# Two DMA queues in place of one for an activation sent across partitions, and a last tile transposed in the middle of a product

## The chip, the core and the metric

The kernel runs on one core of one Trainium2 chip. A core has a matrix engine (PE, with its weight loads shown apart as PEld), a vector engine (DVE), a scalar engine (ACT), GpSimd (POOL) and a sync engine (SP), each with its own queue of instructions. DMAs are issued from the queues of SP, ACT and POOL. The metric is the device time of one launch in microseconds, lower is better.

## The reference

A block of cross-attention with a feed-forward part, then a mixture of experts. The attention part takes 2048 tokens of 256 features as four blocks of 512 and attends to 1601 rows of context. The change is in the mixture of experts alone:

```python
router_logits = x @ wg.T                                   # 8 experts
probs = softmax(router_logits)
topk_w, topk_idx = top_k(probs, 2)
topk_w = topk_w / sum(topk_w)
...
h1 = einsum('th,eih->tei', x, w1)                          # 256 -> 512
h3 = einsum('th,eih->tei', x, w3)
y = einsum('tei,ehi->teh', silu(h1) * h3, w2)              # 512 -> 256
out = einsum('te,teh->th', expert_w, y)                    # only two experts a token count
```

## The kernel before

**The stage.** Up to about 410 us the kernel does the attention and its feed-forward part. From then on it runs the experts. Tokens have been scattered in DRAM (`slots`) into regions by expert, and the stage works through 37 tiles of 128 tokens of one expert each (`sure` is 37): 17 tiles a, 8 tiles p, 12 tiles b. All weights (`wi`, `wo`) lie in SBUF.

**One tile n**, in the loop of `run` (L1337 to L1388):

- `fetch_tile` (L1358) is called for tile n + 3. SP reads the tile's first row from a table into a register (L1149), then issues five DMAs: four for the token rows `xs` (L1155) and a small one for the tokens' weights and numbers, `at` (L1164). `xs` has four buffers.
- `turn_in` (L1189): DVE transposes `xs` in 32 x 32 blocks into `xT`. The loop does this for tile n + 2.
- `hidden` (L1207): PE makes h1 and h3, four matmul instructions each in the profile.
- ACT takes silu of h1 into `g` (L1349, for the last tile L1355), and DVE multiplies `g` by h3 (L1370, last tile L1377).
- `g` has to be transposed, so that its 512 features lie on partitions. For tiles 8 to 35 (`sent`) that takes two steps. `send_across` (L1223) issues four DMAs of 64 KB, SBUF to SBUF, each of which moves a quarter of the features of all 128 partitions into 32 partitions of `gb`. Then `turn_sent` (L1231) lets DVE transpose 32 x 32 blocks into `gT`. The other tiles, tile 36 among them, use `turn_out`: four PE transposes (L1240) and an ACT copy out of PSUM (L1242).
- `product` (L1248): PE multiplies `gT` by `wo` in four steps, eight instructions in the profile. DVE scales the rows (L1256), and POOL adds them to the output with an indirect DMA (L1258).

**Order.** On PE a tile's product comes two tiles late: the order is h1 of tile n, product of tile n - 2, h3 of tile n. From tile 8 on DVE, ACT and SP run in the order of the program text too (`by_hand`, L1341). On DVE that is: scaling of product n - 2, multiplication of tile n, transpose of `gb` of tile n - 1, transpose of `xs` of tile n + 2. On SP only fetches stand. At the end (n = 37) PE does the product of tile 35, the transposes of tile 36, and the product of tile 36. The scatters of L1258 all add to the output, and each starts after the one before it has landed.

Of the kernel before, what the change touches and what calls it, by code (L numbers as in the profile page):

```python
# [19 lines left out]
def xattn_ffn_moe(  # L20
# [21 lines left out]
    nc = tc.nc  # L42
# [11 lines left out]
    NI = I // P  # L54
# [36 lines left out]
    def bank_s(name):  # L91
        return ps_s.tile([P, 512], F32, tag="s", name=name)

    def bank_o(name):
        return ps_o.tile([P, 512], F32, tag="o", name=name)

    def bank_t(name):
        return ps_t.tile([P, 512], F32, tag="t", name=name)
# [872 lines left out]
    def spread(n, run, f, many):  # L971


        le = table(f"le{n}", [many, E])
        nc.vector.tensor_tensor(
            le,
            run.unsqueeze(1).to_broadcast([P, many, E]),
            index[:, :many].unsqueeze(2).to_broadcast([P, many, E]),
            ALU.is_le,
        )  # L980
        ex = table(f"ex{n}", [many])
        nc.vector.reduce_sum(ex, le, axis=AX.X)
        prev = summed(f"prev{n}", le, f.unsqueeze(1).to_broadcast([P, many, E]), [many, E])
        k = table(f"k{n}", [many])
        nc.vector.tensor_sub(k, index[:, :many], prev)
        return ex, k
# [159 lines left out]
    sent = range(SENT, sure - 1)  # L1146
# [49 lines left out]
    def weights_at(ex):  # L1196

        if isinstance(ex, int):
            return ex * WI, ex * WO
        return tuple(  # L1200
            nc.tensor.value_load(a, min_val=0, max_val=(E - 1) * by)
            for a, by in zip(ex, (WI, WO))
        )

    def hidden(name, xT, w, n, into):
        for c in range(ND):
            nc.tensor.matmul(  # L1207
                into,
                lhsT=xT[:, c, :],
                rhs=wi[n, c].rearrange("p e i -> p (e i)")[:, bass.ds(w[0], I)],  # L1210
                start=(c == 0),
                stop=(c == ND - 1),
            )

    def by_quarter(a):

        return a.rearrange("p (c q r) -> p q c r", q=NQ, r=Q)

    def send_across(name, g):

        gb = mp.tile([P, NQ, I // NQ], F32, tag="gb", name=f"gb_{name}")
        for q in range(NQ):
            nc.scalar.dma_start(  # L1223
                gb[q * Q : (q + 1) * Q].rearrange("t i n -> t (i n)"),
                g[:, q * (I // NQ) : (q + 1) * (I // NQ)],
            )
        return gb

    def turn_sent(name, gb):
        gT = mp.tile([P, NI, P], F32, tag="gT", name=f"gT_{name}")  # L1230
        nc.vector.transpose(  # L1231
            gT.rearrange("p c (i t) -> p i c t", t=Q),
            gb.rearrange("p i (c r) -> p i c r", r=Q),
        )
        return gT

    def turn_out(name, g):
        tp = bank_t(f"gtp_{name}")
        for i in range(NI):
            nc.tensor.transpose(tp[:, i * P : (i + 1) * P], g[:, i * P : (i + 1) * P], ident)  # L1240
        gT = mp.tile([P, NI, P], F32, tag="gT", name=f"gT_{name}")
        nc.scalar.copy(gT, tp.rearrange("p (i q) -> p i q", q=P))  # L1242
        return gT

    def product(name, at_token, gT, w, into=out):
        y = bank_o(f"y_{name}")
        for i in range(NI):
            nc.tensor.matmul(  # L1248
                y[:, :D],
                lhsT=gT[:, i, :],  # L1250
                rhs=wo[:, bass.ds(w[1] + i * D, D)],
                start=(i == 0),
                stop=(i == NI - 1),
            )
        yw = mp.tile([P, D], F32, tag="yw", name=f"yw_{name}", bufs=3)
        nc.vector.tensor_scalar_mul(yw, y[:, :D], at_token[:, 0:1])  # L1256
        added.append(
            nc.gpsimd.indirect_dma_start(  # L1258
                out=into,
                out_offset=bass.IndirectOffsetOnAxis(ap=at_token[:, 1:].bitcast(I32), axis=0),  # L1260
                in_=yw,
                in_offset=None,
                compute_op=ALU.add,
            ).ins
        )
        if len(added) in DRAINS:
            with tc.issue_after(added[-1]):
                nc.gpsimd.drain()
# [9 lines left out]
    xs, at_token, xT = {}, {}, {}  # L1278

    def fetch_tile(n):  # L1280
        if n < len(tiles):
            name, row_of, i, _ = tiles[n]
            xs[n], at_token[n] = fetch(n, name, tabs[row_of][0:1, i : i + 1])

    def turn_tile(n):
        if n < len(tiles):
            xT[n] = turn_in(tiles[n][0], xs.pop(n))

    def expert_of(n):
        if n < len(tiles):  # L1290
            _, _, i, ex = tiles[n]
            if isinstance(ex, str):
                i = 0 if ex == "exp" else i
                ex = [a[0:1, i : i + 1] for a in tabs[ex]]
            ws[n] = weights_at(ex)
# [21 lines left out]
    def between(n):  # L1317
        if n == LATE:
            route_at(NB - 1)


        for put in late_puts[:2]:
            with tc.issue_after(added[-1]):
                put()
        del late_puts[:2]
        if n == PUT:
            late_puts.extend(place_at(NB - 1))
            names = ("exb", "rowb", "exp", "rowp", "exr", "rowr", "rare")
            tabs.update(zip(names, tables_b(tabs["done"])))
        if n == NA + E:  # L1330
            tabs["rare"] = nc.values_load(tabs["rare"][0:1, :], min_val=0, max_val=1)  # L1331

    def run(end):


        behind = {}
        for n in range(end + 1):  # L1337
            name = tiles[min(n, end - 1)][0]
            if n == SENT:

                by_hand = {nc.vector.engine, nc.scalar.engine, nc.sync.engine}  # L1341
                ctx.enter_context(tc.manual_schedule(engines=by_hand))
            if n < end:
                w = ws.pop(n)
                h1, h3 = bank_s(f"h1_{name}"), bank_s(f"h3_{name}")
                hidden(name, xT[n], w, 0, h1)
                g = mp.tile([P, I], F32, tag="g", name=f"g_{name}")
                if n in sent:
                    silu = nc.scalar.activation(  # L1349
                        g.rearrange("p (q c r) -> p c q r", q=NQ, r=Q),  # L1350
                        h1.rearrange("p (c q r) -> p c q r", q=NQ, r=Q),
                        AF.Silu,
                    )
                else:
                    silu = nc.scalar.activation(g, h1, AF.Silu)  # L1355
                acted.append(silu.ins)
                if n + AHEAD < end:
                    fetch_tile(n + AHEAD)  # L1358
            if n == end and n - 2 in behind:
                product(*behind.pop(n - 2))  # L1360
            if n - 1 in sent:
                gb = crossed_g
            elif n > 0:
                gT = turn_out(last[0], last[2])
            if n - 2 in behind:
                product(*behind.pop(n - 2))
            if n < end:
                hidden(name, xT.pop(n), w, 1, h3)
                if n in sent:
                    nc.vector.tensor_mul(  # L1370
                        g.rearrange("p (q c r) -> p q c r", q=NQ, r=Q),
                        g.rearrange("p (q c r) -> p q c r", q=NQ, r=Q),
                        by_quarter(h3),
                    )
                    crossed_g = send_across(name, g)
                else:
                    nc.vector.tensor_mul(g, g, h3)  # L1377
            if n - 1 in sent:
                behind[n - 1] = (*last[:2], turn_sent(last[0], gb), *last[3:])
            elif n > 0:  # L1380
                product(last[0], last[1], gT, *last[3:])
            if n < end:
                between(n)
                if n + 2 < end:
                    turn_tile(n + 2)
                if n + 1 < end:
                    expert_of(n + 1)
                last = (name, at_token.pop(n), g, w)  # L1388
# [5 lines left out]
    with tc.If(tabs["rare"] > 0):  # L1394
# [4 lines left out]
        with tc.For_i(0, MORE + E) as i:  # L1399
            xs_r, at_r = fetch(sure, "r", tabs["rowr"][0:1, bass.ds(i, 1)])  # L1400
            xT_r = turn_in("r", xs_r)
            w = weights_at([a[0:1, bass.ds(i, 1)] for a in tabs["exr"]])
# [55 lines left out]
```

## Time and profile before

| what | value |
|---|---|
| time, median of 3 runs | 642.43 us (639.84 to 643.62) |
| the profiled execution | 642.52 us, of which the span on the core is 640.7 us |
| mean granted clock of TensorE | 0.996 |
| expert tiles 8 to 35, product to product (477.93 to 621.60) | 143.67 us, PE busy 140.95 |
| ACT's issues of `gb` | 112, about 0.61 us each |
| DVE transpose of `gb` (L1231) | 0.70 us |
| DVE product (L1370) | 0.69 us |
| transposes of L1231 that waited for `gb` to land | 3.6 us in all, 5 times |
| scatter of L1258, issue to landing | 3.7 to 4.3 us (tiles b) |

How to read the lines shown further on: a line of the order of time has the start (us from the span's start), the length in us, engine and source line, operation, what it writes and reads by the program's names, and in brackets how long the engine had stood idle and what ended that. ACTq and SPq are the queues of ACT and SP; what they issue does not count as busy time of the engine. A line of the waits has who waited for whom, then us in all, times, and the longest.

### The profile page before, as it was taken

How to read it: one execution, taken by the hardware profiler on the slowest of the kernel's cores; microseconds unless marked ns; L12 is line 12 of the kernel's file. 1: busy time of each engine (PE TensorE's matmuls, PEld its weight loads, DVE VectorE, ACT ScalarE, POOL GpSimd, SP SyncE). 2: the span in 40 equal slices, each digit the busy share in tenths (PEclk: the TensorE clock that was granted, in tenths of full speed). 3: DMA queues.
4: the chain of work that ended last, by engine and by line, in shares of the span. 5: the costliest groups of instructions: out<-in, count | busy, mean ns of one | idle time of the engine just before them, and what ended most of it. 6: DMA issues, size and time to landing. Idle time of an engine off the chain costs nothing. (4 is left out here: it accounts for less than half of the span.)

```text
span 640.7 us, 8263 instructions
## 1 busy us (share of the span) xinstructions
PE 623.8 (97%) x2255; PEld 408.8 (64%) x2256; DVE 332.4 (52%) x1011; ACT 141.7 (22%) x251; POOL 169.8 (26%) x240
## 2 busy tenths in 40 slices
PE   9999999999999999999999999999999999999993
PEld 8576745667845687467854688876665555555552
DVE  6662363504274476763587567737743344434341
ACT  3111132123033501352033600334211111111110
POOL 6221100002050032701155022443363222222222
PEclk9999999999999999999999999999999999999998
DMA  8999997001930012200312004953455555555532
GB/s 213 265 250 291 323 246 205 1 0 58 330 105 4 0 28 76 79 20 1 92 37 72 2 13 142 330 153 63 58 103 115 103 97 95 100 105 98 94 76 31
DMA packets 105549, 71.63 MB, mean 112 GB/s; under 512 B 43357, under 2 KB 99870, under 8 KB 105502
## 3 DMA queue, kind: packets, MB, share of 16 engines
q1 hardware_dynamic: 82510, 54.65, 31.9%
q0 software_dynamic: 6864, 9.08, 8.5%
q10 hardware_dynamic: 16128, 7.35, 4.0%
q8 instruction: 20, 0.33, 0.2%
q14 instruction: 27, 0.22, 0.1%
HBM read 28.11 MB, written 29.30 MB: 90 GB/s over the span
## 5 line engine op out<-in xcount | busy, mean ns | idle before, releaser
L233 POOL TENSOR_TENSOR rs<-ve,neghalf 128x1 f32<-128x1 f32 x80 | 47.6, 602 | 214.6 <-DVE ve L231 212.0
L604 PE MATMUL co<-z_sb,raw 128*128 128x257 f32 (+1 forms) x416 | 91.9, 381 | 1.1 <-DVE r L390 1.0
L551 PE MATMUL cs<-yT,zT_sb 128*128 128x512 f32 (+1 forms) x208 | 90.4, 593 | 0.0
L604 PEld LDWEIGHTS co<-z_sb,raw 128*128 128x128 f32 (+1 forms) x416 | 78.6, 190 | 13.0 <-issue 1.9
L551 PEld LDWEIGHTS cs<-yT,zT_sb 128*128 128x128 f32 (+1 forms) x208 | 38.5, 186 | 47.7 <-issue 46.1
L1207 PE MATMUL h_a<-wi,xT_a 128*128 x136 | 62.5, 594 | 0.0
L743 PE MATMUL fo<-w_sb,fhs 128*128 128x256 f32 x256 | 61.1, 380 | 0.0
L494 PE MATMUL acc<-y,pT 128*128 128x257 f32 x252 | 60.2, 381 | 0.8 <-DVE h L392 0.5
L721 PE MATMUL fh<-yT,w_sb 128*128 128x512 f32 (+1 forms) x160 | 60.9, 508 | 0.0
L494 PEld LDWEIGHTS acc<-y,pT 128*128 128x128 f32 x252 | 47.4, 190 | 18.8 <-issue 12.4
L743 PEld LDWEIGHTS fo<-w_sb,fhs 128*128 128x128 f32 x256 | 48.3, 190 | 16.0 <-issue 8.6
L558 ACT COPY raw<-cs 128x512 f32<-128x512 f32 (+1 forms) x52 | 30.4, 585 | 92.9 <-PE cs L551 92.9
L380 PE MATMUL ss<-y0T,y0T 128*128 128x512 f32 x96 | 44.6, 592 | 0.0
L1207 PE MATMUL h_b<-wi,xT_b 128*128 x96 | 43.3, 592 | 0.0
L730 ACT ACTIVATE fhs<-fh,b_sb 128x512 f32<-128x512 f32 (+1 forms) x40 | 24.0, 600 | 81.8 <-PE fh L721 81.8
L721 PEld LDWEIGHTS fh<-yT,w_sb 128*128 128x128 f32 x160 | 30.0, 190 | 17.2 <-issue 13.1
L1258 POOL DMA_INDIRECT out_dram<-yw_a,at_a x17 | 26.6, 1565 | 52.9 <-DVE yw_a L1256 29.4
L363 ACT ACTIVATE pT<-ss 128x512 f32<-128x512 f32 (+3 forms) x37 | 20.8, 562 | 86.8 <-PE ss L380 84.0
L561 DVE TENSOR_TENSOR top<-cs,top 128x512 f32<-128x512 f32 (+1 forms) x44 | 30.2, 687 | 16.9 <-ACT raw L558 16.0
L1207 PEld LDWEIGHTS h_a<-wi,xT_a 128*128 128x128 f32 x136 | 25.1, 190 | 21.8 <-issue 21.0
L1248 PE MATMUL y_a<-wo,gT_a 128*128 x136 | 32.4, 381 | 1.5 <-DVE gT_a L1231 1.5
L1248 PEld LDWEIGHTS y_a<-wo,gT_a 128*128 128x128 f32 x136 | 25.1, 190 | 13.6 <-DVE gT_a L1231 7.1
(267 smaller groups left out, 748.7 us busy)
## 6 DMA issues: line engine op xcount, KB each, us to landing
slots<-empty SPq DMA_DIRECT2D x8, 2064.0 KB
wo<-in_m2T_dram SPq DMA_DIRECT2D x8, 512.0 KB
wi<-in_m1T_dram SPq DMA_DIRECT2D x4, 1024.0 KB
wi<-in_m3T_dram SPq DMA_DIRECT2D x4, 1024.0 KB
gb_b<-g_b ACTq DMA_DIRECT2D x44, 64.0 KB
gb_a<-g_a ACTq DMA_DIRECT2D x36, 64.0 KB
xs_a<-slots SPq DMA_DIRECT2D x68, 32.0 KB
tb_y<-ya SPq DMA_DIRECT2D x16, 128.0 KB
```

The source lines that it names most:

```text
L233: raised.append(nc.gpsimd.tensor_tensor(rs, ve, neghalf, ALU.pow).ins)
L380: nc.tensor.matmul(s, lhsT=y0T[kt // TPB][:, c, (kt % TPB) * P : (kt % TPB + 1) * P], rhs=y0T[b][:, c, j0 * P : j1 * P], start=(c == 0), s ...
L494: nc.tensor.matmul(acc[j][:, : D + 1], lhsT=pt[:, (j - j0) * P : (j - j0 + 1) * P], rhs=y0[kt], start=(kt == 0), stop=(kt == b * TPB + j),)
L551: nc.tensor.matmul(s[:n, :], lhsT=zT_sb[:, c, k * P : k * P + n], rhs=yT[b][:, c, :], start=(c == 0), stop=(c == ND - 1),)
L558: acted.append(nc.scalar.copy(raw[:n, k, :], s[:n, :]).ins)
L561: topped = nc.vector.tensor_tensor(top[:n, :], s[:n, :], raw[:n, 0, :] if k == 1 else top[:n, :], ALU.max).ins
L604: nc.tensor.matmul(acc[j][:, : D + 1], lhsT=raw[:n, k, j * P : (j + 1) * P], rhs=z_sb[:n, k, :], start=(k == 0), stop=(k == NK - 1),)
L721: nc.tensor.matmul(s[:, :n], lhsT=w1_sb[:, c, f * P : (f + 1) * P], rhs=yT[b][:, c, q0 : q0 + n], start=(c == 0), stop=(c == ND - 1),)
L743: nc.tensor.matmul(acc[j], lhsT=h[:, i * P : (i + 1) * P], rhs=w2_sb[:, f, :], start=(f == 0 and i % 2 == 0), stop=(f == NF - 1), skip_gro ...
L1207: nc.tensor.matmul(into, lhsT=xT[:, c, :], rhs=wi[n, c].rearrange("p e i -> p (e i)")[:, bass.ds(w[0], I)], start=(c == 0), stop=(c == ND ...
L1248: nc.tensor.matmul(y[:, :D], lhsT=gT[:, i, :], rhs=wo[:, bass.ds(w[1] + i * D, D)], start=(i == 0), stop=(i == NI - 1),)
L1258: nc.gpsimd.indirect_dma_start(out=into, out_offset=bass.IndirectOffsetOnAxis(ap=at_token[:, 1:].bitcast(I32), axis=0), in_=yw, in_offset= ...
```

## The change

Two edits. First, in `send_across` the four DMAs of a tile are issued from two queues in turn: quarters 0 and 2 from ACT as before, quarters 1 and 3 from SP. Second, the order at the end. In the last iteration with a tile (n = 36) DVE transposes `gb` of tile 35 ahead of the multiplication of tile 36, not behind it. And the PE transposes of tile 36, with their ACT copy, come after the first two of the four steps of tile 35's product, not after all four.

```diff
         for q in range(NQ):
-            nc.scalar.dma_start(
+            (nc.scalar, nc.sync)[q % 2].dma_start(
                 gb[q * Q : (q + 1) * Q].rearrange("t i n -> t (i n)"),
                 g[:, q * (I // NQ) : (q + 1) * (I // NQ)],
             )
...
-    def product(name, at_token, gT, w, into=out):
+    def product(name, at_token, gT, w, into=out, midway=None):
         y = bank_o(f"y_{name}")
         for i in range(NI):
+            if midway and i == NI // 2:
+                midway()
             nc.tensor.matmul(
...
-            if n == end and n - 2 in behind:
-                product(*behind.pop(n - 2))
-            if n - 1 in sent:
+            if n == end:
+
+                turned = []
+                product(
+                    *behind.pop(n - 2),
+                    midway=lambda: turned.append(turn_out(last[0], last[2])),
+                )
+                gT = turned[0]
+            elif n - 1 in sent:
                 gb = crossed_g
             elif n > 0:
                 gT = turn_out(last[0], last[2])
...
             if n < end:
                 hidden(name, xT.pop(n), w, 1, h3)
+                if n == end - 1:
+                    gT = turn_sent(last[0], gb)
                 if n in sent:
...
             if n - 1 in sent:
-                behind[n - 1] = (*last[:2], turn_sent(last[0], gb), *last[3:])
+                if n < end - 1:
+                    gT = turn_sent(last[0], gb)
+                behind[n - 1] = (*last[:2], gT, *last[3:])
             elif n > 0:
                 product(last[0], last[1], gT, *last[3:])
```

## The prediction

> **What bounds the kernel now.** I read the busy shares first, then the PE waits inside the expert stage, then the order of time at its end, then SP's queue.
>
> ```profile
> PE 623.8 (97%) x2255; PEld 408.8 (64%) x2256; DVE 332.4 (52%) x1011; ACT 141.7 (22%) x251; POOL 169.8 (26%) x240
> ...
> PE y_b L1248 <- DVE gT_b L1231: 2.0, 2, 1.5
> PE y_a L1248 <- DVE gT_a L1231: 1.5, 2, 0.8
> PE y_b L1248 <- ACTq L1394: 0.7, 1, 0.7
> PE y_p L1248 <- DVE gT_p L1231: 0.6, 1, 0.6
> ```
>
> PE is the bound, and the change removes no PE work. It can win only where PE stands still: 4.8 us from 476 us on, nearly all for a transposed gT. Now the last tiles, in order of time:
>
> ```profile
> 620.91 0.69 DVE L1370 TENSOR_TENSOR g_b<-g_b,h_b 128x512 f32<-128x512 f32 x1 [1.29 <-PE h_b L1207]
> 621.51 0.70 DVE L1231 STREAM_TRANSPOSE gT_b<-gb_b 128x512 f32<-128x512 f32 x1
> 621.63 2.52 ACTq L1223 DMA_DIRECT2D gb_b<-g_b  x4
> 622.37 1.90 PE L1248 MATMUL y_b<-wo,gT_b 128*128 x8
> 624.11 1.88 PE L1207 MATMUL h_b<-wi,xT_b 128*128 x4
> 626.08 0.69 DVE L1377 TENSOR_TENSOR g_b<-g_b,h_b 128x512 f32<-128x512 f32 x1 [1.29 <-PE h_b L1207]
> 626.68 0.70 DVE L1231 STREAM_TRANSPOSE gT_b<-gb_b 128x512 f32<-128x512 f32 x1
> 627.44 1.99 PE L1248 MATMUL y_b<-wo,gT_b 128*128 x8 [1.46 <-DVE gT_b L1231]
> 629.27 0.60 PE L1240 MATMUL gtp_b<-ident,g_b 128*128 128x128 f32 x4
> 629.91 0.58 ACT L1242 COPY gT_b<-gtp_b 128x512 f32<-128x512 f32 x1 [4.96 <-PE gtp_b L1240]
> 630.24 1.55 POOL L1258 DMA_INDIRECT out_dram<-yw_b,at_b  x1 [3.63 <-DVE yw_b L1256]
> 630.55 1.99 PE L1248 MATMUL y_b<-wo,gT_b 128*128 x8 [0.67 <-ACTq L1394]
> 635.28 1.54 POOL L1258 DMA_INDIRECT out_dram<-yw_b,at_b  x1 [3.49 <-issue]
> ```
>
> The reader is to see three things. An undisturbed tile takes 5.17 us (two products earlier, at 617.20, PE started the one that here starts at 622.37). The four sends of one tile keep ACT's queue for 2.52 us. And the last scatter starts at 635.28, 2.2 us after its rows were ready (632.58 + 0.48): it waits for the scatter of 630.24 to land. The chain of waits says the same, running from that scatter's DMA straight to the end.
>
> **Two queues, the gain.** Of the four issues of a tile (median 0.615 us, 0.65 from one to the next) two go to SP. Both queues are released by the same DVE product, so the last issue starts about 0.65 us after it, not 1.93. In the trace's semaphore times a piece lands 2.2 us after its issue; the last piece thus lands 2.85 us after the product, not 4.1. The transpose that needs it comes 5.1 us after the product, behind the next product on DVE, so in an undisturbed tile nothing is won: slack grows from 1.0 to 2.25 us.
>
> What can be won are the disturbed tiles. From the product of tile 8 (ends 477.93) to that of tile 35 (621.60) 143.67 us pass; 27 x 5.17 are 139.6. The 4.1 us between lie in five tiles that took 5.5 to 6.2 us. In the trace's packets I find, just before four of them, a 16,384-byte instruction packet (513.8: 0.95 us; 481.0: 1.7; 545.3: 1.1; 581.4: 1.5) with some gb packets held behind it on one DMA engine; the piece caught landed 3.8 to 4.4 us after its issue. With all four pieces issued within 1.25 us most have moved before such a packet comes, and those caught have 1.2 us more to spare. I take 3.6 of the 4.1 us; bounds 0 (others get caught) and 4.1.
>
> A rule of the Trainium skill speaks against this. "DMA: Bandwidth & Descriptors", Issuing engines are not separate DMA queues, says that starting DMAs from several engines saves only the sequencer's issue time, "which is usually small relative to the DMA itself". By the rule the gain would be near 0. By the row, issuing is 2.5 of the 4.1 us from product to last landing, so I go by the row; the rule holds in that the 2.2 us of transfer stay.
>
> **Two queues, the price: SP.** SP today only fetches tiles, and where nothing held it, it ran freely:
>
> ```profile
> 458.29 1.87 SPq L1155 DMA_DIRECT2D xs_a<-slots  x4
> 460.41 0.62 SPq L1164 DMA_DIRECT2D at_a<-slots  x1
> 462.35 1.86 SPq L1155 DMA_DIRECT2D xs_a<-slots  x4
> ...
> L293 SPq DMA_DIRECT2D tb_y<-ya x48: 547/601/6482, 35.0 to 403.7; - x48
> ```
>
> One fetch costs 4.06 us free (458.29 to 462.35), 4.5 where ACT issues at the same time (the four xs then take 2.33). It has two ends in it that matter: the register load of L1149 takes 0.73 us here, against 0.27 (median) for the early tiles' loads. To this come two sends. SP has sent such blocks before, SBUF to SBUF, 32 partitions by four: 0.55 and 0.60 us, the L293 row, 1.25 us with gaps. So SP would need 4.06 + 1.25 = 5.3 us a tile, more than the 5.17 that PE takes. This is the step on which the sign hangs. It now blocks in order too: the fetch of tile n+4 stands behind the wait for product n, where before SP ran five tiles ahead.
>
> Two corrections. The long register load: every 0.73 us load comes right behind the small at DMA in its later form (0.62 us); behind other DMAs (wi, the early at of 0.35 us) it is 0.28 to 0.29. The same page, Why a DMA increments its semaphore by 16 and not by 1, says that a DMA on k < 16 engines leaves the sequencer to write the other 16 - k increments. That fits the 0.62 against 0.35 us, and the later at has 4 closing packets where xs and gb have 16. In the new order the load comes behind gb, which has 16, so by the rule it costs 0.28 and SP needs 4.85 us. By the row alone, 0.73, it is 5.3. The other correction: SP's sends now run beside ACT's; beside ACT's issues xs rose from 0.32 to 0.47, so up to 0.3 for the pair. Bounds: 4.85 to 5.75 us a tile. I take 5.0, the short load and half of the contention, below 5.17 with little to spare.
>
> Were it more, the lag adds up over 26 tiles (8 to 33, the last ones fetch nothing), and 2.25 us of it cost nothing. Tile 34's sends on SP start at 26 C behind those of tile 8, land 2.85 later, and its transpose then starts at 26 C + 2.95, against 143.58 now. Break-even for the loop is C = 5.41.
>
> The fetches themselves: xs of tile n+4 is issued by 4.4 us behind product n, lands 2 us on, and is turned 11 us behind it. No wait there. ACT's silu comes up to 1.3 us earlier; its reader waits for PE, so nothing. No added PE work; the POOL scatters (3.8 us to landing, then 0.7) fit in 5.17.
>
> **The last tile.** (a) The transpose of tile 35 goes ahead of product 36 on DVE. DVE is free from 624.79 (the scaling of L1256) to 626.08; gb of tile 35 would be there at 621.60 + 2.85 = 624.45, so it runs 624.8 to 625.5 and delays nothing. If it landed over 0.9 us late, product 36 and all behind it would move. PE's 1.46 us gap goes: product 35 starts at 625.99, when the hidden features end. (b) Half of product 35 (1.0) to 627.0; g of tile 36 is there at 626.77 + 0.06; four transposes (0.60) to 627.6; second half (0.95) to 628.55, covering ACT's copy (0.58, done at 628.25); the last product 628.55 to 630.55, not 632.54. So PE ends 2.0 us earlier.
>
> What is late next is the scatter chain. Scatter 35 needs product 35, which the transposes hold up by 0.6: 628.55 + 0.04 + 0.48 + 0.28 = 629.35 instead of 630.24 (scatter 34 lands at 628.80, in time). It lands 3.8 to 4.3 us on; scatter 36 starts 0.74 after that. Its own rows are ready at 631.1, long before. Of PE's 2.0 us only **0.9** reach the end, up to 1.4 if scatter 35 lands in the usual 3.8.
>
> **Sum.** The profiled execution took 642.52 us (span 640.70 and 1.82 around it), the median of the runs is 642.43. 642.5 - 3.6 - 0.9 = **638.0 us**.
>
> **Rivals.**
> 1. *SP becomes the bound.* The register load stays at 0.73 and the contention is paid: C = 5.6. Loop: 26 x 5.6 + 2.95 - 143.58 = +4.95; the tail gives back 0.9: **646.5**. It decides for slower from C = 5.45 on. For it: the free-running cycle plus the L293 row is 5.3 without any contention, and SP's xs issues were held for 1.4 and 1.7 us at two of the instruction packets. Against it: the short loads behind other DMAs.
> 2. *Only the tail counts.* The stalls of the loop stay: SP's lag eats the slack that the second queue made (C about 5.4), or the instruction packets catch other pieces. 642.5 - 0.9 = **641.6**. For it: in undisturbed tiles the landing is not late at all. Against it: four of the five long tiles have a late landing.
> 3. *The end gains all of PE's 2.0 us*, loop as forecast: 636.9. Against it: the last scatter waits for the one ahead of it, not for its rows.
>
> **Chances.** Forecast and rival 3 together 0.45, rival 2 0.22, rival 1 0.33. Within 0.5% (3.2 us; about what a measurement here can tell from no change) is rival 2. Forecast alone: 636.5 to 639.3. The range over all, 636.5 to 646.5, cuts off the upper half of rival 1, which reaches to 650 at C = 5.75.
>
> **What would show it.** Right: the waits for gT on L1231 fall from 4.1 to under 1 us, SP's queue stands idle between an at and the next gb, xs starts every 5.17 us; at the end PE's last product starts near 628.5 less what the loop gained, with no gap ahead of it, and the last scatter still starts over 2 us behind its rows. Wrong: xs starts 5.4 us or more apart, the SP half of gb starts later and later behind its product, DVE waits for gb in tile after tile and PE behind it. What would overturn all of it is a DMA on SP that waits for another queue's landing, which the trace of before cannot show.

## The result, and the profile after

The changed kernel is slower: 651.58 us in the median (651.05 to 653.52) beside 641.13 for the kernel before, a ratio of 1.0156 (95% interval 1.0136 to 1.0175). The profiled execution has a span of 650.2 us, 9.5 more than before. The share of busy time and the waits of PE for a transposed `gT` in the expert stage (waiting engine, line and its releaser; us in all, times, longest):

```profile
PE 627.4 (96%) x2255; PEld 408.3 (63%) x2256; DVE 334.1 (51%) x1011; ACT 141.7 (22%) x251; POOL 169.6 (26%) x240
...
PE y_b L1250 <- DVE gT_b L1231: 3.8, 3, 2.5
PE y_p L1250 <- DVE gT_p L1231: 2.9, 8, 0.7
PE y_a L1250 <- DVE gT_a L1231: 1.7, 3, 1.0
```

Before, PE waited so at 5 of the 28 sent tiles; now it does at 14, all 8 of the p tiles among them. What DVE waits for is in its own waits, at 18 tiles:

```profile
DVE gT_b L1231 <- DMA gb_b<-g_b: 5.0, 5, 2.7
DVE gT_p L1231 <- DMA gb_p<-g_p: 3.8, 7, 0.9
DVE gT_a L1231 <- DMA gb_a<-g_a: 2.9, 6, 1.2
```

That is 11.7 us for sends that have not landed, against 3.6 before. From the product of tile 8 to that of tile 35 153.5 us pass now, 143.7 before: the loop lost 9.8 us, the end gave back 0.7 (from the start of the last DVE product, that of tile 36, to the end of the span 13.97 us, before 14.63), and 0.3 more passed ahead of tile 8. Why the sends land late is seen on SP's queue, in order of time (start, length, line, what is issued, how many):

```profile
504.77 2.12 SPq L1155 DMA_DIRECT2D xs_a<-slots  x4
507.14 0.69 SPq L1164 DMA_DIRECT2D at_a<-slots  x1
507.94 1.23 SPq L1223 DMA_DIRECT2D gb_a<-g_a  x2
510.56 2.09 SPq L1155 DMA_DIRECT2D xs_p<-slots  x4
512.90 0.69 SPq L1164 DMA_DIRECT2D at_p<-slots  x1
513.69 1.23 SPq L1223 DMA_DIRECT2D gb_a<-g_a  x2
516.29 2.22 SPq L1155 DMA_DIRECT2D xs_p<-slots  x4
```

The reader is to see that SP never pauses. A pair of sends starts 0.11 us after the small `at` DMA ends, and the next pair 5.75 us later. The holes of 1.4 us between a pair and the next `xs` are register work, mostly the load of L1149:

```profile
L1149 SPq TENSOR_LOAD <-rowb_i x12: 274/820/851, 555.1 to 619.4; - x12
L1149 SPq TENSOR_LOAD <-rowp_i x8: 807/818/830, 509.2 to 549.1; - x8
L1149 SPq TENSOR_LOAD <-rowa_i x5: 819/823/827, 479.6 to 503.5; - x5
```

(ns, least, median, most.) The load takes 0.82 us, not 0.28. From the pair of tile 8 (478.22) to that of tile 33 (623.52), 25 rounds on, a round of SP takes 5.81 us on average, above PE's 5.17. By tile 11 a pair already starts 3.0 us behind its product.

### The profile page after: what moved, and what is told of

It is laid out like the page before. It is cut to its first block, busy times and chain, and to the rows that moved or that the text cites. A ratio compares the mean times of both kernels' runs of the same rounds, so it can differ in the third digit from the quotient of the medians.

```text
span 650.2 us, 8283 instructions
## 1 busy us (share of the span) xinstructions
PE 627.4 (96%) x2255; PEld 408.3 (63%) x2256; DVE 334.1 (51%) x1011; ACT 141.7 (22%) x251; POOL 169.6 (26%) x240
```

## The experiments

Theory A: SP's time for one tile (fetch and sends) is longer than PE's, and becomes the period. Rivals: the new order at the end costs; or it is not SP's time, but that its queue now stands behind the wait for each product, with the sends in one ring behind the fetches (rival B). All edits are against the changed kernel, but for the first, which is against the kernel before. "Loop" is from the product of tile 8 to that of tile 35 in the profiled execution.

| run | ratio to before (95%) | loop, us |
|---|---|---|
| before | 1 | 143.7 |
| changed | 1.0156 (1.0136 to 1.0175) | 153.5 |
| e1: two queues alone | 1.0190 (1.0156 to 1.0223) | 154.6 |
| e2: the end alone | 0.9984 (0.9969 to 1.0000) | 141.5 |
| e10: the same again | 0.9984 (0.9970 to 0.9997) | 142.6 |
| e3: one send in four from SP | 0.9965 (0.9953 to 0.9977) | 139.9 |
| e9: the same again | 0.9958 (0.9943 to 0.9973) | 139.9 |
| e4: register load behind xs | 1.0046 (1.0026 to 1.0067) | 150.9 (its slowest run) |
| e5: at from ACT | 0.9984 (0.9963 to 1.0004) | 142.0 |
| e6: three sends in four from SP | 1.0393 (1.0356 to 1.0430) | 168.0 |
| e7: at in plain order (mixes tokens up) | 0.9973 (0.9958 to 0.9989) | 140.8 |
| e8: at in four DMAs, one run | 677.28 us beside 642.21 | 178.1 |

**e1 and e2, the two parts apart.**

```diff
-            nc.scalar.dma_start(                          # e1: only this
+            (nc.scalar, nc.sync)[q % 2].dma_start(
...
-            (nc.scalar, nc.sync)[q % 2].dma_start(        # e2: only this taken back
+            nc.scalar.dma_start(
```

> The two queues alone, the end as before. Theory A (SP needs more time for a tile, fetch plus two sends, than PE does, and its time becomes the period): all of the loss and the gain of the end missing, 651 to 652.5 us, SP's register loads 5.5 to 5.9 us apart. Rival (the new order at the end costs, or shares in the loss): 645 or less.

> The end alone, all sends from ACT. Theory A: the loop is as before, the end gains what the changed kernel's end gained, 0.6 us, up to 1.4: 639.8 to 640.6 us. Rival (the new order at the end costs): slower than before, 642 or more.

Measured 653.72 and 640.12 us, beside 641.44. The queues carry all of the loss (1.2 us more than the upper number expected), and the end alone gains about 1.0 us by its ratio; e10, the same kernel again, excludes that it costs anything.

**e3, one send in four from SP.**

```diff
-            (nc.scalar, nc.sync)[q % 2].dma_start(
+            (nc.sync if q == NQ - 1 else nc.scalar).dma_start(
```

> As changed, but only quarter 3 from SP, three from ACT. Theory A: SP is 0.63 us a tile lighter, 5.81 - 0.63 = 5.2 us, at PE's own 5.17; the loop runs at PE's pace and the stalls of before mostly go: 636.5 to 640 us. Rival B (not SP's time, but that SP's queue now stands behind the wait for each product and its sends lie in one ring behind the fetches): that wait is still there for every tile, so most of the loss stays, 646 us or more.

Measured 638.90 us. The wait for every product is still in SP's queue, and yet nothing is lost, so the wait alone is not the cause. That two sends in SP's ring could cost what one does not is left to e5. Here is all that PE still waits for in the expert stage, and a stretch of SP's queue:

```profile
PE y_b L1250 <- DVE gT_b L1231: 0.2, 1, 0.2
```

```profile
517.31 1.86 SPq L1155 DMA_DIRECT2D xs_p<-slots  x4
519.43 0.65 SPq L1164 DMA_DIRECT2D at_p<-slots  x1
520.18 0.64 SPq L1223 DMA_DIRECT2D gb_a<-g_a  x1
522.19 1.86 SPq L1155 DMA_DIRECT2D xs_p<-slots  x4
```

A round takes 4.88 us (517.31 to 522.19), so SP catches up after a disturbed tile instead of falling further behind. The stalls of before are gone, and the loop runs at 139.9 us, near the 139.6 of 27 tiles at 5.17.

**e4, the register load moved.** SP loads the next tile's row right behind the `xs` DMAs.

```diff
-        r = nc.sync.value_load(at, min_val=0, max_val=DUMMY)
+        r = rows_ahead.pop(n) if n in rows_ahead else row_at(at)
...
+        if at_next is not None:
+            rows_ahead[n + 1] = row_at(at_next)
```

> As changed, two sends from SP, but SP reads the next tile's row right behind the four xs DMAs, and not behind the sends (0.82 us there); the small at DMA goes ahead of xs. Same DMAs, same wait. Theory A with a load that is short behind xs (0.28): 5.81 - 0.54 = 5.27 us a tile, 638 to 642 us. Theory A with a load that is long behind any DMA of this stage: 5.7 to 5.8 a tile, 650 to 652. Rival B (order and ring, not SP's time): no change, 650 to 652 whatever the load takes.

Measured 644.71 us (639.88 to 650.42), between the two numbers expected. The profiled execution is the slowest of these, with a round of SP of 5.55 us on average, and nothing here explains the wide spread. The load has neither of the lengths I had named:

```profile
L1151 SPq TENSOR_LOAD <-rowb_i x12: 458/517/781, 551.8 to 612.5; - x12
L1151 SPq TENSOR_LOAD <-rowp_i x8: 457/464/1103, 506.7 to 546.0; - x8
```

With 0.46 it saves 0.36 us a tile, and the time falls by 7 us without any DMA or wait being taken away, though `at` now goes ahead of `xs`. That speaks for A and leaves open what the load waits for.

**e5, e6 and e7: SP made lighter and heavier.**

```diff
+            by = nc.scalar                                # e5, tiles 11 to 36
+            ra = nc.scalar.value_load(at, min_val=0, max_val=DUMMY)
+            of_at = slots[bass.ds(ra, P), :]
...
-            (nc.scalar, nc.sync)[q % 2].dma_start(        # e6
+            (nc.scalar if q == 0 else nc.sync).dma_start(
...
-        order = "(t i) n -> i t n" if n in sent else "(i t) n -> i t n"   # e7
+        order = "(i t) n -> i t n"
```

> As changed, two sends from SP and two from ACT, but the small at DMA of a fetch (0.69 us with 0.25 ahead of it on SP) is issued from ACT for tiles 11 to 36, with a register load of its own there. Theory A (SP's time is the period): SP needs 5.81 - 0.94 = 4.9 us a tile, under PE's 5.17: 637 to 640 us, as with one send in four. Rival (two sends on SP's ring, behind the fetches, are what makes the loss, and one was below some limit): 646 or more.

> As changed, but three sends from SP and one from ACT. Theory A: 5.81 + 0.65 = 6.46 us a tile on SP; by the prediction's formula (26 C + 2.95 - 143.58, and 0.6 back at the end) 27 us above before: 665 to 670 us. Rival (SP's wait in order costs once a tile, however many sends follow it): about as the changed kernel, 650 to 655.

> As changed, but at is fetched in its plain order for every tile, which takes 0.35 us on SP and not 0.69; the rows of tiles 8 to 35 get each other's weights and numbers, so this part of the output differs. Theory A: 5.81 - 0.34 = 5.47 us a tile, 641.5 to 645 us; the register load behind the sends stays at 0.82, since it is the sends that it follows. If the load is long because of at's form: 0.3 there, 4.95 a tile, 637 to 640 us.

They ran beside a kernel before of 645.49 us, so the ratios count. e6 came to 1.0393, 25.4 us above before, where the formula had said 27: with a send more a round of SP takes 6.33 us on average, and DVE waits for `gb` at 23 of the 28 tiles:

```profile
DVE gT_b L1231 <- DMA gb_b<-g_b: 11.0, 8, 3.1
DVE gT_p L1231 <- DMA gb_p<-g_p: 7.5, 8, 1.2
DVE gT_a L1231 <- DMA gb_a<-g_a: 7.1, 7, 1.3
```

e5 has the two sends on SP and no loss, so rival B falls. It also shows that the long load goes with the `at` DMA. SP's loads, with no `at` in the queue, are short, and those on ACT, which now issues `at`, are long:

```profile
L1149 SPq TENSOR_LOAD <-rowp_i x8: 271/294/352, 509.6 to 545.8; - x8
L1166 ACTq TENSOR_LOAD <-rowp_i x8: 742/818/1095, 510.0 to 546.1; - x8
```

e5 gains less than expected. On ACT the `at` DMA takes 1.1 us to issue, and tile 8 alone took 6.85 us in its profiled execution, with PE waiting 1.0 us for ACT's copy of tile 7, ahead of which the first of these DMAs stands.

e7, a probe whose tokens of tiles 8 to 35 get each other's weights and numbers, settles the load. It falls on the side of "because of at's form", which I had not thought likely, since two sends lie between `at` and the load:

```profile
L1149 SPq TENSOR_LOAD <-rowb_i x12: 271/284/455, 550.4 to 607.4; - x12
L1149 SPq TENSOR_LOAD <-rowp_i x8: 266/286/430, 507.9 to 544.5; - x8
L1149 SPq TENSOR_LOAD <-rowa_i x5: 263/274/297, 482.1 to 502.7; - x5
```

Same place, same two sends ahead of it, 0.28 us. Without the block-ordered `at` a round of SP takes 4.54 us where it is not waiting (pairs at 518.17 and 522.71).

**e8, what it is about at.** The block order could cost because its rows lie apart, or because the DMA runs on few engines.

```diff
+            by_i = of[:, D:].rearrange("(t i) n -> i t n", i=NQ)
+            gets += [
+                nc.sync.dma_start(at_token[i * Q : (i + 1) * Q], by_i[i]).ins
+                for i in range(NQ)
+            ]
```

> As changed, but the block-ordered at of tiles 8 to 35 is fetched by four DMAs of 32 partitions each in place of one. The values are the same. If at's cost (0.69 us, and a register load of 0.82 after it) comes from running on 4 DMA engines only, each of the four takes 0.35 us and the load 0.28, though the rows read are as far apart as before: about 5.81 - 0.54 - 0.94 + 4 x 0.54 = 6.5 us a tile on SP, some 670 us. If it comes from reading every fourth 8-byte row, each takes 0.69 and the load stays at 0.8: 8.4 us a tile, 715 us or more.

```profile
L1166 SPq DMA_DIRECT2D at_p<-slots x32: 315/326/1107, 515.4 to 566.1; - x32
...
L1149 SPq TENSOR_LOAD <-rowp_i x8: 264/272/278, 512.4 to 561.4; - x8
```

The same distant rows, in four DMAs of 32 partitions: 0.33 us each, and a load of 0.27. So the distance of the rows is not it, and the number of engines is the likely cause; no run here changes that number alone. In the changed kernel's trace the semaphore of the block-ordered `at` gets five updates, the first 1.1 us after the issue starts and the last after 2.2; each of the four DMAs of e8 gets 16. That agrees with a write by the sequencer and four engines, as in the Trainium skill, "DMA: Bandwidth & Descriptors", Why a DMA increments its semaphore by 16 and not by 1: the issuing sequencer itself writes the increments of the engines that a DMA does not use. What that writing costs no run here shows apart. The time, 677.28 us in one run, fits a round that measured 6.7 us.

**e9 and e10, the better version again.**

> The version with one send in four from SP once more, five rounds, beside the next: 0.9965 of before again, within 0.2%.

> The end alone once more, five rounds: 0.998 to 0.999 of before, so that the send in four is worth 1 to 2 us on top of it. If the two are level, the stalls of the loop cost less in most runs than in the profiled one.

Measured 638.44 and 640.56 us, beside 642.21. One send in four from SP with the new end beats both kernels: 0.9958 of before (0.9943 to 0.9973). That is 2.5 to 3.8 us in the medians; beside e10, which has the new end and all sends from ACT, it is 2.1. Both are less than the 4.8 us between the profiled executions of before and e3, and the loops in the table say why. With all four sends from ACT the loop took 143.7 us in the profile of before, but 141.5 and 142.6 in those of e2 and e10, and with one send in four from SP it took 139.9 twice. The profile of before had more stalls than the other two of its kind.

## Why the prediction was wrong

- **The bound and the stalls** were read rightly. In e3, where SP keeps up, the loop loses 3.8 of its 4.1 us of stalls; the prediction took 3.6. As a usual gain that is too much, since it was read from one execution: beside the loops of e2 and e10, 1.6 and 2.7 us are won.
- **The price on SP is where it failed**, in the correction to the register load: "In the new order the load comes behind gb, which has 16, so by the rule it costs 0.28 and SP needs 4.85 us. By the row alone, 0.73, it is 5.3." It costs 0.82. I had taken the load to be long only right behind the block-ordered `at`; two sends later it is as long (e7 against the changed kernel). The rule cited there is about what the sequencer writes for the small DMA; how long the effect on a later load lasts was my addition, and no row of before showed it. The row at hand, 0.73, with the same 0.15 for contention, makes C = 4.06 + 1.25 + 0.15 = 5.46, and the formula then loses 1.3 us in the loop and wins 0.9 at the end: about level. The load's 0.54 alone decides the sign, for without it the measured 5.81 would be 5.27, below the break-even of 5.41.
- **The other terms of the 5.0 us.** The four `xs` take 2.07 us (median) and not 1.86. SP is late, and in all 25 rounds they overlap ACT's next sends; in e3, where they do so in 2 rounds of 25, they take 1.86. So contention may be there, but not where I had put it: the pair of sends takes 1.23, where 1.25 and 0.15 more had been taken. `at` takes 0.69 and not 0.62. 5.0 + 0.54 + 0.21 + 0.07 - 0.17 makes 5.65; the median round is 5.75, and disturbed ones bring the mean to 5.81, just above the upper bound of 5.75.
- **Rival 1** was the mechanism, with its formula but for one round. Tile 33's sends are the last with a fetch ahead of them, 25 rounds after tile 8's, and before, its transpose started 138.42 us after the product of tile 8. So 25 x 5.81 + 2.95 - 138.42 is 9.8 us for the loop, and 9.8 were measured; the prediction's 26 rounds make 10.4. For e6 the formula gave 27 in all, with a round of 6.46; 25.4 came, with 6.33. Rival 1's own time of 646.5 was too low because it used 5.6.
- **The landing** was right: a send from SP landed 2.2 us after its issue (median), one from ACT before 2.3. Being issued some 3 us late, the second of a pair landed 5.9 us after its product.
- **The end** was right in kind: 0.9 forecast, 0.7 in the changed kernel's profile, 1.0 by the ratios of e2 and e10. Counted from the product of tile 35, PE ends 2.35 us earlier (8.60 us, before 10.95; 2.0 were forecast), and the last scatter starts only 1.1 us earlier (12.54, before 13.68), since it still waits for the one before. From its start to the end of the span 5.9 us pass, 5.4 before (5.3 to 6.0 in the runs here), which takes part of the gain back. The end after the change, in order of time:

```profile
636.07 1.13 PE L1250 MATMUL y_b<-wo,gT_b 128*128 x4
637.03 0.60 PE L1240 MATMUL gtp_b<-ident,g_b 128*128 128x128 f32 x4
637.47 2.83 PE L1250 MATMUL y_b<-wo,gT_b 128*128 x12
638.54 0.48 DVE L1258 TENSOR_SCALAR yw_b<-y_b,at_b 128x256 f32<-128x256 f32 x1 [1.65 <-PE y_b L1250]
639.74 1.55 POOL L1260 DMA_INDIRECT out_dram<-yw_b,at_b  x1 [3.02 <-DVE yw_b L1258]
640.34 0.48 DVE L1258 TENSOR_SCALAR yw_b<-y_b,at_b 128x256 f32<-128x256 f32 x1 [1.32 <-PE y_b L1250]
644.24 1.54 POOL L1260 DMA_INDIRECT out_dram<-yw_b,at_b  x1 [2.95 <-issue]
```

The second half of tile 35's product and the whole of tile 36's run on without a gap (x12). What I had missed is that the scatter at 639.74 waits as well: its rows were ready at 639.02, 0.7 us earlier, where 0.28 is the usual step, but the scatter before it, issued at 635.17, takes about 3.8 us to land, and the next starts 0.74 us after that. By the prediction's own terms, 628.80 and 0.74, it could start at 629.54 at the soonest and not at 629.35. All three last scatters stand in one chain. And with all sends from ACT (e2, e10) the danger shows that the prediction named under (a): DVE waits 1.0 to 1.1 us for tile 35's `gb` ahead of product 36, which comes 5.5 us behind product 35 and not 5.17.

## What to carry to other kernels

Before work is moved to another queue, add up what one round of that queue takes, gaps and register loads included, and set it beside the period of the bound: an issuer that seems to be ahead by five tiles may be so only because its round is a fifth shorter (here 4.06 us against 5.17). Where the sum lies within some tenths of a microsecond of the bound, a step that rests on an effect no row shows (here that a load gets shorter in a new place) should not decide the sign. If the idea is sound and the queue nearly full, move less of it: one send in four was enough to free the loop of its stalls.

## What was not expected of the hardware

- A small DMA in the block order, 128 pieces of 8 bytes, takes 0.62 to 0.69 us to issue on SP and makes a later register load of the same queue long: 0.73 us right behind it (before), 0.82 with two sends between them, 0.46 with four `xs` between them, 0.28 where the data came in plain order (0.35 us to issue) or in four DMAs (0.33 each). What the load waits for inside the queue was not found. Once in the changed kernel another register load stands ahead of that of L1149, and then that one is long, while the load of L1149 behind it takes 0.27 us; the time falls on the first load behind the small DMA (in e6 the second still took 0.54):

```profile
L1333 SPq TENSOR_LOAD <-rare_i x1: 806/806/806, 578.1 to 578.1; - x1
```

- Where SP and ACT issue sends at the same moment, ACT's second takes 0.84 us in the median of e5 and 0.86 in that of e7, in place of 0.61, while SP's second stays at 0.60. With one send in four on SP (e3) ACT's sends stay at 0.62.
